# A graph layer on one core: the last but one node group's products behind the last pair's sum

## The chip, the cores and the metric

The kernel runs on one core of a Trainium2 chip. What counts is the time of one execution on the device, in microseconds (us), as the median of three runs. A separate execution was taken with the hardware profiler, and all readings of the trace come from it.

## The reference

One layer of graph attention (GATv2) with a feed-forward block, on 12,500 nodes of 128 features and 400,000 edges sorted by their destination. Every node has a self loop besides.

```python
h0 = relu(layernorm(x))
hn = LN(h0; ln1)
x_l, x_r, e = hn @ W_l, hn @ W_r, edge_attr @ W_e          # 8 heads of 16
m     = leaky_relu(x_l[src] + x_r[dst] + e, 0.2)           # a self loop's e is the mean over all edges
alpha = einsum(m, att)                                     # one score for each edge and head
a     = softmax of alpha over the edges of one destination
h     = h0 + segment_sum(x_l[src] * a, dst) + bias
out   = x + h + gelu(LN(h; ln2) @ W1 + b1) @ W2 + b2
```

All of it is in float32.

## The kernel before

A first stage computes the rows x_l for all nodes and puts them in DRAM. The main stage (window_edges) walks over the edges in 782 **pairs** of 512 edges (four tiles of 128; the last pair, 781, has one tile). Because the edges are sorted, a pair touches few nodes, and its result is a small record, rec, that is written with two DMAs into one of two state arrays in DRAM (L1073). Two writes into the same state array wait for each other.

The work of the main stage is written out by hand in **rounds**. Round r does one stage each of several pairs: GpSimd gathers the source rows xs of pair r + 4 (L926), one indirect DMA a tile; TensorE turns and sums pair r (combine, L980 and L984), starts the scores of pair r - 2 (apart, L991), turns the weights of pair r - 4 (L1033), sums pair r - 6 (collect, L1047) and ends the scores of pair r - 2 (score, L1008). VectorE takes the heads of pair r - 7 (own and rec, L1056 and L1062), the lowest score of pair r - 3 (L1014), the larger of z and its slope of pair r - 1 (m, L1003), and the places of pair r + 1 (ea and, every second round, ne, L967 and L973). ScalarE copies turned weights (L1038), slopes z (L998) and takes exponentials p (L1025). SP, which only issues DMAs, loads windows for pair r + 3 and writes the records of pair r - 7. Each engine works strictly in the order in which the code issues its instructions, and a waiting instruction holds all behind it on its engine. A few pairs are kept rows: their xs is loaded from late_dram by SP instead (pair 776 is the last of these).

PSUM has four rings of two banks each: z, ab, pt_ps and acc. An instruction that takes a new bank of a ring waits until the last use of the bank two before it is done. There are 12 buffers for xs.

Beside the pairs, the nodes are finished in **groups** of four tiles of 128 nodes (the first and the last have three), once the edges into them are done. A group's steps are: load its rows (f_load: three DMAs), self loop (f_order, f_z, f_bend, f_score, and f_kept, which copies the scores out of PSUM so that their bank comes free), read of both state arrays (f_state), weights (f_low, f_exp, f_den), weighted sum (f_out, which holds an ab bank until f_h is through), residual (f_h), statistics (f_stats, f_root, f_scale), turn (f_turn, f_turned), the two products and gelus (up0, up1, gelu0, gelu1), the product back (f_down), the result (f_store) and its DMA (f_put). A table for each kind of group says in which round, counted from the group's own, a step is issued: steps for all but the last two, which have one step a round; soon for the last but one, whose own round is 772; last_steps for the last, whose own round is 790, behind the last pair's sum in round 787 and its state writes in rounds 788 and 789.

f_biases adds the bias to h_sb and b2 to x ahead of time. In before only the last group has it; the others add them in f_h and in f_store. f_rest adds h_sb to x ahead of f_store, and f_ready is a Gelu of one column that makes ScalarE load the Gelu table early.

At the end of each round the tables are called in this order:

```python
in_round(r, steps, groups[:-2])
in_round(r, soon, groups[-2:-1])
in_round(r, last_steps, groups[-1:])
```

Of the kernel before, what the change touches and what calls it, by code (L numbers as in the profile page):

```python
# [851 lines left out]
def window_edges(  # L852
# [30 lines left out]
    with ExitStack() as es:  # L883
# [218 lines left out]
        groups = [{"t0": t, "n": n, "ts": slice(t, t + n)} for t, n in node_groups(NT)]  # L1102
        end = groups[-1]

        def own_tile(d, name, shape, dt, tag=None, bufs=1):

            if d is end and name in ("xo", "x", "sc"):
                return fin.tile(shape(d["n"]), dt, name=f"end_{name}")
            return fin.tile(shape(GN), dt, name=f"f_{name}", tag=tag or f"f_{name}", bufs=bufs)

        def tiles(name, d, tag=None):
            d[name] = own_tile(d, name, lambda n: [P, n, P], F32, tag)
            return d[name][:, 0 : d["n"]]

        def bank_of(d, name, ring="acc"):
            d[name] = ps2.tile([P, EPR], F32, name=ring)
            return d[name]
# [110 lines left out]
        def f_h(d):  # L1228
            hb = h_sb[:, d["ts"], :].rearrange("p t f -> p (t f)")
            nc.vector.tensor_add(d["sum"], d["sum"], d["o2"])  # L1230
            if d is not end:
                up = d["sum"].rearrange("p (t f) -> p t f", f=P)
                nc.vector.tensor_add(up, up, bias_r[:, None, :].to_broadcast([P, d["n"], P]))
            nc.vector.tensor_add(hb, hb, d["sum"])
# [31 lines left out]
                )  # L1266

        def f_turn(d):
            tp = bank_of(d, "tp")
            for i in range(d["n"]):  # L1270
                nc.tensor.transpose(tp[:, i * P : (i + 1) * P], d["hn"][:, i, :], ident)

# [20 lines left out]

        def f_up(k):
            def up(d):
                n, u = d["n"], bank_of(d, f"u{k}")
                nc.tensor.matmul(  # L1297
                    u[:, 0 : n * P],
                    w1_sb[:, k * P : (k + 1) * P],
                    d["hT"][:, 0:n].rearrange("p t f -> p (t f)"),  # L1300
                    start=True,
                    stop=True,
                )

            return up

        def f_gelu(k):
            def gelu(d):
                n = d["n"]
                if k == 0:  # L1310
                    d["gel"] = own_tile(d, "gel", lambda n: [P, 2, n * P], F32, "big", 3)
                nc.scalar.activation(
                    d["gel"][:, k, 0 : n * P], d[f"u{k}"][:, 0 : n * P], AF.Gelu, bias=cols[:, 5 + k : 6 + k]
                )

            return gelu

        def f_down(d):
            y = bank_of(d, "y")
            for i in range(d["n"]):  # L1320
                for k in range(2):
                    nc.tensor.matmul(  # L1322
                        y[:, i * P : (i + 1) * P],
                        d["gel"][:, k, i * P : (i + 1) * P],
                        w2_sb[:, k, :],
                        start=(k == 0),
                        stop=(k == 1),
                    )

        def f_store(d):  # L1330
            n = d["n"]
            up = d["y"][:, 0 : n * P].rearrange("p (t f) -> p t f", f=P)
            d["out"] = y = tiles("yo", d, "f_b")
            if d is end:
                nc.vector.tensor_add(y, up, d["x"][:, 0:n])
                return
            nc.vector.tensor_add(up, up, d["x"][:, 0:n])
            nc.vector.tensor_add(up, up, h_sb[:, d["ts"], :])
            nc.vector.tensor_add(y, up, b2_r[:, None, :].to_broadcast([P, n, P]))

        def f_put(d):
# [51 lines left out]
        )  # L1393
        up0, up1, gelu0, gelu1 = f_up(0), f_up(1), f_gelu(0), f_gelu(1)
        soon = (
            (-4, f_load),
            (-3, f_order),
            (-2, f_z),
            (-1, f_bend),
            (0, f_state),  # L1400
            (0, f_score),
            (1, f_low),
            (1, f_exp),
            (2, f_den),
            (2, f_out),
            (3, f_h),
            (3, f_stats),
            (4, f_root),
            (4, f_scale),
            (5, f_turn),  # L1410
            (5, f_turned),
            (6, up0),
            (6, gelu0),
            (7, up1),
            (7, gelu1),
            (8, f_down),
            (9, f_store),
            (9, f_put),
        )
        last_steps = (  # L1420
            (-18, f_load),
            (-17, f_order),
            (-16, f_z),
            (-15, f_bend),
            (-15, f_biases),
            (-14, f_score),
            (-13, f_kept),
            (0, f_state),
            (1, f_low),
            (1, f_exp),  # L1430
# [41 lines left out]
        with tc.manual_schedule():  # L1472
            for r in range(-AHEAD, max(last_round, groups[-1]["round"] + 18)):
                in_round(r, early, groups[:-2])
                for late, f in stages:
                    c = r - late
                    if 0 <= c < n_pr:
                        f(c)
                for late, f in sum_stages:
                    i, off = divmod(r - late, SUM_STEP)  # L1480
                    if off == 0 and 0 <= i < NL:
                        f(i)
                if r > 0 and r % CLEAR == 0 and r // CLEAR < NT // GT:
                    clear(r // CLEAR)
                in_round(r, steps, groups[:-2])
                in_round(r, soon, groups[-2:-1])
                in_round(r, last_steps, groups[-1:])
                in_round(r, enumerate(xr_steps), qs[1:])
                in_round(r, enumerate(raw_steps), raw)
                for late, f in late_stages:  # L1490
                    c = r - late
                    if 0 <= c < n_pr:
                        f(c)
# [354 lines left out]
```

## Time and profile before

| | us |
|---|---|
| median of 3 runs | 3979.37 (3976.93 to 3980.35) |
| profiled execution | 3979.82 |
| its span | 3978.0 |
| busy TensorE (matmul) | 3535.5 (89%) |
| busy VectorE | 2996.7 (75%) |
| busy GpSimd | 2961.1 (74%) |
| busy ScalarE | 2177.6 (55%) |
| mean granted clock of TensorE | 0.955 |

The 1.8 us between the profiled execution and its span lie outside what the profile shows. GpSimd's busy time leaves out the short pause before each gather. In the rows of a timeline the columns are start, duration, engine, line, operation, output and inputs, count, and in brackets the idle time before it and what ended it. In the rows of the chain that ended last they are start, duration and what the time went to. A stretch's row gives, for PE, PEld, DVE, ACT and POOL, the busy time and in brackets the instructions, then TensorE's granted clock, the DMA share and GB/s.

### The profile page before, as it was taken

What the parts mean: (1) busy time and instruction counts of PE and PEld (TensorE: products, weight loads), DVE (VectorE), ACT (ScalarE), POOL (GpSimd) and SP (SyncE); (2) the same over time, 40 slices, a digit from 0 to 9 for tenths busy, and PEclk for the clock granted to TensorE, in tenths of its full rate; (3) what the DMA queues carried; (4) which work ended last, traced back from release to release, by engine and by line L of the source; (5) the groups of instructions that cost most, each with busy time, mean ns of one, the idle gap of its engine ahead of it and who ended that gap; (6) DMA issues with size and microseconds to landing.
All of it is one profiled execution on the core that took longest, in us unless ns stands there. A gap on an engine that the chain in (4) does not pass through costs nothing.

```text
span 3978.0 us, 63158 instructions
## 1 busy us (share of the span) xinstructions
PE 3535.5 (89%) x18434; PEld 2235.4 (56%) x18435; DVE 2996.7 (75%) x6282; ACT 2177.6 (55%) x4746; POOL 2961.1 (74%) x3147
## 2 busy tenths in 40 slices
PE   2588899999999999999999999989999999999987
PEld 2355555555555556555665556656565655555554
DVE  6578888888878777777777777777777767767766
ACT  7445545555555545555555555556455555555554
POOL 7777777777777777777777777777777777777772
PEclk9799999999999999999999999999999999999998
DMA  7677777766655555555555555555555555555552
GB/s 207 210 176 175 182 190 179 165 161 154 151 103 114 109 112 112 109 110 108 104 110 115 109 110 111 113 109 108 112 104 107 110 115 97 110 110 100 107 104 63
DMA packets 625309, 502.69 MB, mean 126 GB/s; under 512 B 320174, under 2 KB 522013, under 8 KB 624717
## 3 DMA queue, kind: packets, MB, share of 16 engines
q1 hardware_dynamic: 524381, 281.11, 29.6%
q0 software_dynamic: 100000, 217.32, 27.7%
q8 instruction: 152, 2.49, 0.3%
q14 instruction: 200, 1.64, 0.1%
q10 hardware_dynamic: 576, 0.13, 0.0%
HBM read 432.27 MB, written 65.83 MB: 125 GB/s over the span
## 4 chain that ended last, share of the span: by engine, by line
PE 41%; POOL 20%; DMA 17%; issue 13%; DVE 7%; ACT 1%; SPq 1%; POOLq 0%; DVEq 0%; ACTq 0%
POOL xs L926 17%; DMA xs<-xl_dram,src_sb 14%; PE acc L1047 10%; PE z L984 10%; PE ab L1008 8%; PE pt_ps L1033 7%; PE z L980 4%; POOL raw L288 2%; DVE rec L1014 1%; DMA state<-rec 1%; DVE ea L967 1%; DVE m L1003 1%; PE acc L1322 1%; PE acc L1297 1%; DVE own L1056 1%
## 5 line engine op out<-in xcount | busy, mean ns | idle before, releaser
L926 POOL DMA_INDIRECT xs<-xl_dram,src_sb x3009 | 2842.4, 945 | 917.3 <-issue 790.1
L1025 ACT ACTIVATE p<-ab,rec 128x256 f32<-128x256 f32 x1563 | 654.8, 470 | 1026.9 <-DVE rec L1014 1011.6
L1047 PE MATMUL acc<-xs,pt 128*128 128x136 f32 x6250 | 904.6, 291 | 0.6 <-DVE f_m L1166 0.5
L984 PE MATMUL z<-ea,zw 64*128 64x512 f32 x1564 | 900.4, 656 | 3.8 <-DMA zw<-xr_dram 3.5
L980 PE MATMUL z<-ident,xs 128*128 128x128 f32 x3125 | 575.9, 285 | 291.0 <-DMA xs<-xl_dram,src_sb 260.3
L1056 DVE TENSOR_TENSOR own<-acc,diag 128x272 f32<-128x272 f32 x782 | 342.9, 438 | 652.5 <-PE acc L1047 646.5
L1008 PE MATMUL ab<-m,negrep 128*128 128x512 f32 x1564 | 833.5, 616 | 0.0
L1047 PEld LDWEIGHTS acc<-xs,pt 128*128 128x128 f32 x6250 | 828.8, 201 | 1.1 <-DVE f_m L1166 0.8
L980 PEld LDWEIGHTS z<-ident,xs 128*128 128x128 f32 x3125 | 406.9, 144 | 718.2 <-DMA xs<-xl_dram,src_sb 370.8
L1038 ACT COPY pt<-pt_ps 128x512 f32<-128x512 f32 x782 | 454.8, 582 | 573.1 <-PE pt_ps L1033 562.1
L1033 PEld LDWEIGHTS pt_ps<-ident,p 128*128 128x128 f32 x3125 | 340.5, 145 | 617.9 <-issue 510.1
L1003 DVE TENSOR_TENSOR m<-z,zs 128x512 f32<-128x512 f32 x782 | 532.8, 681 | 103.6 <-ACT zs L998 99.1
L967 DVE TENSOR_SCALAR ea<-dl,nid 32x516 f32<-32x516 bf16 x782 | 582.1, 744 | 29.0 <-DMA dl<-dc_dram 3.7
L1014 DVE TENSOR_REDUCE rec<-ab 128x2 f32<-128x512 f32 x781 | 538.8, 690 | 34.8 <-PE ab L1008 33.4
L1033 PE MATMUL pt_ps<-ident,p 128*128 128x128 f32 x3125 | 534.4, 296 | 2.6 <-ACT pt L1038 1.9
L998 ACT ACTIVATE zs<-z 128x512 f32<-128x512 f32 x782 | 472.0, 604 | 45.4 <-PE z L984 45.4
L1062 DVE TENSOR_REDUCE rec<-own 128x34 f32<-128x272 f32 x782 | 340.8, 436 | 26.7
L991 PE MATMUL ab<-ne,farw 64*128 64x512 bf16 x782 | 307.3, 393 | 31.2 <-ACT p L1025 27.4
L984 PEld LDWEIGHTS z<-ea,zw 64*128 64x128 f32 x1564 | 234.7, 188 | 122.3 <-issue 59.8
L1008 PEld LDWEIGHTS ab<-m,negrep 128*128 128x128 f32 x1564 | 252.8, 200 | 2.3 <-issue 2.3
L973 DVE TENSOR_SCALAR ne<-dl,nid 96x512 bf16<-96x512 bf16 x391 | 145.7, 373 | 12.7 <-DMA dl<-du_dram 0.3
L288 POOL DMA_INDIRECT raw<-in_x,src_raw x116 | 115.3, 994 | 38.8 <-issue 34.4
(206 smaller groups left out, 2163.2 us busy)
## 6 DMA issues: line engine op xcount, KB each, us to landing
ea<-in_ea_t SPq DMA_DIRECT2D x392, 128.0 KB
ea_s<-in_ea_t SPq DMA_DIRECT2D x98, 512.0 KB
xs<-xl_dram,src_sb POOLq DMA_INDIRECT x3009
dl<-dc_dram SPq DMA_DIRECT2D x392, 66.0 KB
state<-rec SPq DMA_DIRECT2D x1563, 9.0 KB
state<-empty SPq DMA_DIRECT2D x28, 504.0 KB
f_st<-state SPq DMA_DIRECT2D x46, 288.0 KB
dl<-du_dram SPq DMA_DIRECT2D x392, 32.0 KB
```

The source lines that it names most:

```text
L926: nc.gpsimd.indirect_dma_start(out=xs[:, j, :], out_offset=None, in_=xl_dram, in_offset=bass.IndirectOffsetOnAxis(ap=src_sb[:, c * KP + j ...
L967: nc.vector.tensor_scalar(d["ea"][rs].rearrange("p (a b) -> p a b", b=OW), d["dl"][rs].rearrange("p (a b) -> p a b", b=OS)[:, :, 0:OW], ni ...
L980: nc.tensor.matmul(z[:, j * P : (j + 1) * P], d["xs"][:, j, 0:P], ident, start=(j == 0), stop=False, is_transpose=True)
L984: nc.tensor.matmul(z[:, :e], d["zw"][rs], d["ea"][rs, :e], start=False, stop=True)
L998: nc.scalar.activation(d["zs"][:, :e], d["z"][:, :e], AF.Copy, scale=SLOPE)
L1003: nc.vector.tensor_tensor(d["m"][:, :e], d["z"][:, :e], d["zs"][:, :e], op=OP.max)
L1008: nc.tensor.matmul(d["ab"][:, :e], negrep.rearrange("p n h -> p (n h)"), d["m"][:, :e], start=False, stop=True)
L1014: nc.vector.tensor_reduce(d["rec"][:, :, CX], d["ab"].rearrange("p (u e) -> p u e", e=U), AX.X, OP.min)
L1025: nc.scalar.activation(d["p"][:, us], d["ab"][:, us], AF.Exp, bias=d["rec"][:, i, CX:SH], scale=-1.0)
L1033: nc.tensor.transpose(d["pt_ps"][:, js], d["p"][:, js], ident)
L1038: nc.scalar.copy(d["pt"][:, :e], d["pt_ps"][:, :e])
L1047: nc.tensor.matmul(d["acc"][:, i, :], d["pt"][:, j * P : (j + 1) * P], d["xs"][:, j, :], start=(j == js[0]), stop=(j == js[-1]),)
```

## The change

The last but one group (groups[-2]) changes its table. In soon, its loads and its self loop move from rounds 768 to 772 up to rounds 758 to 763, with f_biases and f_kept added; f_low stays in round 773; f_exp, f_den, f_out, f_h, f_stats, f_root and f_scale, which shared rounds 773 to 776 in twos and threes, get rounds 774 to 780, and f_rest is added in round 780. Its turn, products, gelus, product back, result and put leave rounds 777 to 781. They form a new table, after, and are counted from the last group's round 790: f_ready and the turn in round 788, the products and gelus in 789, f_down and f_store in 790, f_put in 791. Their PSUM banks come from the rings z and ab instead of acc. The last group's self loop moves from rounds 772 to 777 up to 764 to 769.

```diff
+        def near_end(d):
+            return any(d is g for g in groups[-2:])
+
...
-            if d is not end:
+            if not near_end(d):
                 up = d["sum"].rearrange("p (t f) -> p t f", f=P)
                 nc.vector.tensor_add(up, up, bias_r[:, None, :].to_broadcast([P, d["n"], P]))
...
-            tp = bank_of(d, "tp")
+            tp = bank_of(d, "tp", "z" if d is groups[-2] else "acc")
...
-                n, u = d["n"], bank_of(d, f"u{k}")
+                n, u = d["n"], bank_of(d, f"u{k}", "z" if d is groups[-2] else "acc")
...
-            y = bank_of(d, "y")
+            y = bank_of(d, "y", "ab" if d is groups[-2] else "acc")
...
-            if d is end:
+            if near_end(d):
                 nc.vector.tensor_add(y, up, d["x"][:, 0:n])
                 return
...
         soon = (
-            (-4, f_load),
+            (-14, f_load),
...
+        after = (
+            (-2, f_ready),
+            (-2, f_turn),
...
         last_steps = (
-            (-18, f_load),
+            (-26, f_load),
...
                 in_round(r, soon, groups[-2:-1])
+                for k, f in after:
+                    if end["round"] + k == r:
+                        f(groups[-2])
                 in_round(r, last_steps, groups[-1:])
```

In the changed kernel the lines below the new function are 3 higher, so that L1271, L1297, L1322 and L1342 are L1274, L1300, L1325 and L1345 there.

On TensorE, before, at the end of round 777 and over round 778, the turn (L1271) and the first product (L1297) stand between the pairs' instructions:

```order
5743 L1047 MATMUL acc<-xs,pt 128x136 x4
5744 L1008 MATMUL ab<-m,negrep 128x512
5745 L1271 MATMUL acc<-ident,f_hn 128x128 x4
5746 L980 MATMUL z<-ident,xs 128x128 x4
5747 L984 MATMUL z<-ea,zw_1772 128x512
5748 L991 LDWEIGHTS farw
5749 L991 MATMUL ab<-ne_1773,farw 128x512
5750 L1033 MATMUL pt_ps<-ident,p 128x128 x4
5751 L1047 MATMUL acc<-xs,pt 128x136 x4
5752 L1008 MATMUL ab<-m,negrep 128x512
5753 L1297 MATMUL acc<-f_hT,w_sb 128x512
```

On TensorE, after, at the end of the program:

```order
5783 L1033 MATMUL pt_ps<-ident,p 128x128 x4
5784 L1047 MATMUL acc<-xs,pt 128x136 x4
5785 L1033 MATMUL pt_ps<-ident,p 128x128
5786 L1047 MATMUL acc<-xs,pt 128x136 x9
5787 L1274 MATMUL z<-ident,f_hn 128x128 x4
5788 L1300 MATMUL z<-f_hT,w_sb 128x512 x2
5789 L1325 MATMUL ab<-w_sb,f_gel 128x128 x8
5790 L1274 MATMUL acc<-ident,f_hn 128x128 x3
5791 L1300 MATMUL acc<-f_hT,w_sb 128x384 x2
5792 L1325 MATMUL acc<-w_sb,f_gel 128x128 x6
```

The three rows of the four-tile group now stand between the last pairs' sums (L1047) and the last group's own three.

On SP, before, the put of the group (128x4x128) stands between the state writes, eight pairs from their end:

```order
4349 L1073 DMA state_69<-rec 128x72
4350 L1073 DMA state_70<-rec 128x72
4351 L1073 DMA state_69<-rec 128x72
4352 L1073 DMA state_70<-rec 128x72
4353 L1342 DMA out<-f_yo 128x4x128
4354 L1073 DMA state_69<-rec 128x72
4355 L1073 DMA state_70<-rec 128x72
```

On SP, after, at the end of the program:

```order
4367 L1073 DMA state_69<-rec 128x72
4368 L1073 DMA state_70<-rec 128x72
4369 L1073 DMA state_69<-rec 128x72
4370 L1126 DMA f_st<-state_69 128x3x144
4371 L1126 DMA f_st<-state_70 128x3x144
4372 L1345 DMA out<-f_yo 128x4x128
4373 L1345 DMA out<-f_yo 128x3x128
```

It has moved behind the last group's two state reads and stands right ahead of the last put.

On VectorE, after, at the end of the last pair's records, the group's result (L1338) now stands ahead of the last group's first step (L1190):

```order
6095 L1056 TENSOR_TENSOR own<-acc,diag 128x136
6096 L1062 TENSOR_REDUCE rec<-own 128x17
6097 L1338 TENSOR_TENSOR f_yo<-ab,f_x 128x512
6098 L1190 TENSOR_TENSOR f_mn<-f_st 128x24
6099 L1191 TENSOR_TENSOR f_mn<-f_mn,end_sc 128x24
```

In before it stood in three adds (L1337 to L1339) between the records of round 781.

More of the change, by code (lines that the diff above doesn't have):

```diff
@@ L1395, in window_edges @@
         soon = (
-            (-4, f_load),
-            (-3, f_order),
-            (-2, f_z),
-            (-1, f_bend),
+            (-14, f_load),
+            (-13, f_order),
+            (-12, f_z),
+            (-11, f_bend),
+            (-11, f_biases),
+            (-10, f_score),
+            (-9, f_kept),
             (0, f_state),
-            (0, f_score),
             (1, f_low),
[L1403 to L1418, printed above, removed]
+            (2, f_exp),
+            (3, f_den),
+            (4, f_out),
+            (5, f_h),
+            (6, f_stats),
+            (7, f_root),
+            (8, f_scale),
+            (8, f_rest),
+        )
+        after = (
+            (-2, f_ready),
+            (-2, f_turn),
+            (-2, f_turned),
+            (-1, up0),
+            (-1, up1),
+            (-1, gelu0),
+            (-1, gelu1),
+            (0, f_down),
+            (0, f_store),
+            (1, f_put),
         )
         last_steps = (
-            (-18, f_load),
[L1422 to L1427, printed above, removed]
+            (-26, f_load),
+            (-25, f_order),
+            (-24, f_z),
+            (-23, f_bend),
+            (-23, f_biases),
+            (-22, f_score),
+            (-21, f_kept),
             (0, f_state),
```

## Prediction

> **What bounds the kernel now.** The page first: GpSimd's gathers carry the loop.
>
> ```profile
> span 3978.0 us, 63158 instructions
> L926 POOL DMA_INDIRECT xs<-xl_dram,src_sb x3009 | 2842.4, 945 | 917.3 <-issue 790.1
> ```
>
> 945 ns busy and 917.3 / 3009 = 305 ns of idle before each make 1.25 us a gather, 5.0 us a pair of four. The timeline of GpSimd keeps that step to its end (columns: start, duration):
>
> ```profile
> 3895.36 0.94 POOL L926 DMA_INDIRECT xs<-xl_dram,src_sb  x1 [0.30 <-issue]
> ...
> 3915.62 0.94 POOL L926 DMA_INDIRECT xs<-xl_dram,src_sb  x1 [0.30 <-issue]
> 3916.87 0.94 POOL L926 DMA_INDIRECT xs<-xl_dram,src_sb  x1 [0.30 <-issue]
> ```
>
> These are the last gathers of pairs 775, 780 and 781 (pair 781 has one tile; pair 776 is a kept one that GpSimd doesn't gather). They never wait for a row tile. So nothing behind 3917.8 us can be won on GpSimd: 60.2 us of tail are left. How long a gather takes to land, from the chain that ended last:
>
> ```profile
> 3725.39 3.71 DMA xs<-xl_dram,src_sb
> ...
> 3885.37 5.41 DMA xs<-xl_dram,src_sb
> ```
>
> The second is pair 773: it lands at 3890.78, just as TensorE asks for it, so at round 773 TensorE has no arrears. Pair 781 lands at 3916.87 + 3.7 to 5.4 = 3920.6 to 3922.3. TensorE's timeline says when it is used:
>
> ```profile
> 3897.42 1.02 PE L1008 MATMUL ab<-m,negrep 128*128 128x512 f32 x2
> 3900.96 0.52 PE L1152 MATMUL acc<-ident,f_xl 128*128 128x128 f32 x3 [2.52 <-issue]
> ...
> 3918.52 0.63 PE L1271 MATMUL acc<-ident,f_hn 128*128 128x128 f32 x4 [2.33 <-DVE end_sc L1178]
> ...
> 3937.39 0.27 PE L980 MATMUL z<-ident,xs 128*128 128x128 f32 x1
> ...
> 3946.65 2.25 PE L1047 MATMUL acc<-xs,pt 128*128 128x136 f32 x18
> ```
>
> 3897.42 is the score that ends round 774; 3937.39 is pair 781's turn, 15 to 17 us behind its landing; the last sum ends at 3948.90 (call this moment S), 11.5 us later. So between 3890 and 3937 TensorE, not GpSimd, sets the end, and the arrears arise there: two stalls of 2.52 and 2.33 us while VectorE does the last but one group's steps, the group's own products, and a low clock, which the stretches show:
>
> ```profile
> 3920.00:3927.00 7.00, 7.00 (x18) 3.92 (x17) 3.01 (x5) 2.95 (x5) 0.00 (x0) 0.53 0.05 5
> ```
>
> TensorE is busy for all 7.00 us at a granted clock of 0.53: 7.0 x (1 - 0.53) = 3.3 us lost.
>
> **Part by part.** *Products moved behind the last sum.* Their steps in the chain that ended last:
>
> ```profile
> 3918.52 0.63 PE acc L1271 x4
> ...
> 3925.90 1.29 PE acc L1297 x2
> ...
> 3931.04 0.86 PE acc L1297 x2
> ...
> 3935.77 1.78 PE acc L1322 x16
> ```
>
> 0.63 + 0.86 + 0.86 + 1.78 = 4.13 us leave TensorE's path ahead of S (the 1.29 is the 0.86 at the low clock). With them two Gelu loads and the two Exp loads behind them leave ScalarE's rounds; ScalarE isn't what TensorE waits for there.
>
> *VectorE's steps, one a round instead of two or three.* These are VectorE's rows around the first stall (round 775 starts at 3900.78), and the last exponential of its round on ScalarE:
>
> ```profile
> 3893.76 0.44 DVE L1056 TENSOR_TENSOR own<-acc,diag 128x272 f32<-128x272 f32 x1 [0.88 <-PE acc L1047]
> 3896.72 0.28 DVE L1201 TENSOR_TENSOR f_ws<-f_wt,f_st 128x64 f32<-128x64 f32 x1
> 3898.25 0.70 DVE L1214 TENSOR_TENSOR ab<-f_st,acc 128x512 f32<-128x512 f32 x1
> 3900.78 0.43 DVE L1056 TENSOR_TENSOR own<-acc,diag 128x272 f32<-128x272 f32 x1
> 3902.31 0.84 ACT L1025 ACTIVATE p<-ab,rec 128x256 f32<-128x256 f32 x2 [4.54 <-DVE rec L1014]
> 3903.95 0.69 DVE L1230 TENSOR_TENSOR ab<-ab,f_o 128x512 f32<-128x512 f32 x1
> ```
>
> A round's own work takes 2.96 us (3893.76 to 3896.72), or 3.17 in the rounds that also place ne (3900.78 to 3903.95); f_den 1.53; f_out 2.53; from a round's start to its last p it is 3903.15 - 3900.78 = 2.37. In before, f_den and f_out together stand between two rounds (4.06 us). Apart they fit better, but f_out still puts 2.53 us into round 776. It also takes an ab bank, so that apart of round 777 must wait for p of round 777. An earlier group, whose steps already come one a round, shows this very wait, and what followed:
>
> ```profile
> 3754.31 0.60 PE L980 MATMUL z<-ident,xs 128*128 128x128 f32 x4
> 3758.32 0.37 PE L991 MATMUL ab<-ne,farw 64*128 64x512 bf16 x1 [2.36 <-ACT p L1025]
> 3760.67 1.91 PE L1008 MATMUL ab<-m,negrep 128*128 128x512 f32 x2
> 3762.38 0.81 PE L980 MATMUL z<-ident,xs 128*128 128x128 f32 x4
> 3765.59 1.02 PE L1008 MATMUL ab<-m,negrep 128*128 128x512 f32 x2
> 3769.45 1.02 PE L1008 MATMUL ab<-m,negrep 128*128 128x512 f32 x2
> ```
>
> A free round takes 3769.45 - 3765.59 = 3.86 us. That one took 3762.38 - 3754.31 = 8.07: 3.86 + 2.36 of waiting + 1.85 at a low clock (the score took 1.91 instead of 1.02).
>
> Now the rounds of after. Round 774 as before, its score done at 3898.3. Round 775 waits for its pair, 3895.36 + 3.7 to 5.4 = 3899.1 to 3900.8; from a landing to the end of a round it is a free round, so it ends at 3903.0 to 3904.7. Round 776 has its pair: 3906.9 to 3908.5. VectorE enters round 776 with the sum of 775, 0.86 before that round's end, at 3902.1 to 3903.8; + 3.17 + 2.53 it enters 777 at 3907.8 to 3909.5, and p is there at + 2.37: 3910.2 to 3911.9. TensorE reaches apart some 0.9 us into its round 777, at 3907.8 to 3909.4, and waits 2.4 to 2.5 us, as the earlier group did. The round then needs another 2.97 (3.86 - 0.9): 3913.2 to 3914.9. Three rounds of 3.86 bring pair 781's turn to 3924.8 to 3926.4; its landing by 3922.3 doesn't hold it. Against 3937.39 that is 11.0 to 12.6 us earlier, and 9.1 to 10.7 if the low clock takes 1.85 again. From there to S the same pairs have the same 11.5 us of TensorE.
>
> [...]
>
> *Self loops of both groups earlier* (rounds 758 to 769): six loads past state writes and window loads on SP, two copies, two ScalarE slopes, two f_m, four bias adds on VectorE, two f_z and f_score on TensorE, and one f_kept more. I cost them at nothing: there TensorE waits for gathers, at most this long:
>
> ```profile
> 3863.54 0.33 PE L980 MATMUL z<-ident,xs 128*128 128x128 f32 x1 [1.90 <-DMA xs<-xl_dram,src_sb]
> ...
> 3880.80 1.06 PE L1156 MATMUL acc<-ident,f_xr 128*128 128x128 f32 x8
> ```
>
> and it gets back rounds 770 to 776, which lose their f_z (about 1.5 us for four tiles) and f_score. If that cover is gone, arrears of some us come into round 774; a free round gains 5.0 - 3.86 = 1.1 us on the gathers.
>
> *Behind S.* What the moved group must not delay:
>
> ```profile
> 3948.25 0.43 DVE rec L1062
> ...
> 3948.94 1.43 DMA state<-rec
> ```
>
> ```profile
> 3953.52 0.93 SPq L1123 DMA_DIRECT2D f_st<-state  x2
> ...
> 3956.88 0.20 DVE L1187 TENSOR_TENSOR f_mn<-f_st 128x24 f32<-128x24 f32 x1 [6.72 <-DMA f_st<-state]
> ```
>
> f_mn starts 8.0 us after S, after three state writes one behind the other, the first 0.26 us behind its rec: SP has caught up with what its wait on f_put had held, so taking that wait away gives nothing. The moved chain, from S: turn 0.63, f_hT, two products of 0.86, the second gelu, the second half of L1322 at most 1.78, one add:
>
> ```profile
> 3919.18 0.78 ACT L1286 ACTIVATE f_hT<-acc,cols 128x512 f32<-128x512 f32 x1 [0.61 <-PE acc L1271]
> ...
> 3932.35 0.69 ACT L1312 ACTIVATE f_gel<-acc,cols 128x512 f32<-128x512 f32 x1
> ...
> 3937.77 0.69 DVE L1337 TENSOR_TENSOR acc<-acc,f_x 128x512 f32<-128x512 f32 x1
> ```
>
> 0.63 + 0.78 + 1.72 + 0.69 + 1.78 + 0.69 = 6.3, with some 0.04 at each handing on 6.6. f_mn, queued behind that add on VectorE, has 1.4 us to spare; at half the clock TensorE's 4.13 us more would take 2.7 of it too much. The clock is still full there:
>
> ```profile
> 3953.00:3954.00 1.00, 0.00 (x0) 0.00 (x0) 0.00 (x0) 0.00 (x0) 0.00 (x0) 0.97 0.03 2
> ```
>
> it falls only 5 us after S. The Exp load lies in the same gap on ScalarE. f_put stands behind the state loads on SP and holds only the last put. The rest of the tail, 21.1 us from f_mn, keeps its order. Two adds of f_store and one of f_h are gone from VectorE (0.69 each); no wait of TensorE hangs on them.
>
> Sum: 11.8 us (middle of 11.0 to 12.6), less 1.85 for the low clock = 9.95. The profiled run takes 3979.82 (span and 1.8 around it), 0.45 over the median of 3979.37: 3979.82 - 9.95 - 0.45 gives a median of 3969.4.
>
> **The rivals.**
>
> - *No low clock.* The 2.4 us wait passes as the 2.52 us one did: 3979.4 - 11.8 = 3967.6. For it one idle in three; against it the closest twin.
> - *A longer loss.* The low clock lasts as in 3920 to 3927 (3.3 us), or pair 780 lands late, or VectorE stays behind: gain 7 to 8.5, time 3971 to 3972.5.
> - *Only the products are won.* The stalls come back at other rounds, as arrears from rounds 758 to 772: gain 4.13, time 3975.2. For it: VectorE works 9.59 of the 10 us at 3900, in this row, and its sum of work hardly falls:
>
> ```profile
> 3900.00:3910.00 10.00, 8.50 (x50) 5.76 (x51) 9.59 (x25) 2.39 (x5) 7.55 (x9) 1.00 0.29 62
> ```
>
> - *Slower.* The loads and VectorE steps at rounds 758 to 769 hold TensorE so long that GpSimd finds no free row tile (12 of them, filled 4 rounds ahead, emptied 6 rounds behind), and its last gather slips. Each us it stands costs one us of the end; it decides only once it passes the 10 us won, and slower by 8 us needs 18, some 3.6 pairs. Against it: GpSimd's idle stays at 0.30 even beside the low clock near 3866. Time 3987 and up.
> - *No change:* the moved chain holds f_mn at half the clock (2.7 us) and rival three holds too: 3978.
>
> **How the numbers follow.** Three runs differ by 3.4 us, and 0.2% is 8.0 us, about what a measurement can tell. Forecast 0.42, no low clock 0.26, longer loss 0.13 (half of it over 8.0), only products 0.11, slower 0.05, no change 0.03. Faster: 0.42 + 0.26 + 0.06 = 0.74; same: 0.07 + 0.11 + 0.03 = 0.21; slower 0.05. The range runs from 3966.0, where apart of round 777 would wait for nothing (11.0 + 2.4 = 13.4 us), to 3975.5, which takes in the third rival.
>
> **What would show it.** GpSimd's last gather still at 3916.9; pair 781's L980 at 3925 to 3928; one wait of L991 on p near 3908; the low clock, if any, right behind it and none at 3920; S at 3936 to 3939; f_yo's add done before f_st lands, f_mn 8 us after S. I am wrong if GpSimd's end moves, if f_mn comes later than 8.3 us after S, or if TensorE waits for VectorE in rounds 778 to 781.

## The result and the profile after

The changed kernel takes 3971.46 us (median; 3967.20 to 3974.63), the kernel before 3978.16 us beside it on the same chip (3975.27 to 3981.08), 21 times each. The medians are 6.7 us apart (0.17 %); the ratio of the runs is 0.9981 with an interval of 0.9975 to 0.9987. The profiled execution took 3973.0 us, its span is 3971.2 us.

On the page GpSimd's gathers are what they were:

```profile
span 3971.2 us, 63157 instructions
...
L926 POOL DMA_INDIRECT xs<-xl_dram,src_sb x3009 | 2843.4, 945 | 917.4 <-issue 772.6
```

TensorE's timeline of the changed kernel from round 777 on (start, duration, and in brackets the idle time before):

```profile
3908.80 0.60 PE L980 MATMUL z<-ident,xs 128*128 128x128 f32 x4
...
3912.99 0.37 PE L991 MATMUL ab<-ne,farw 64*128 64x512 bf16 x1 [2.54 <-ACT p L1025]
...
3915.45 1.91 PE L1008 MATMUL ab<-m,negrep 128*128 128x512 f32 x2
3917.16 0.70 PE L980 MATMUL z<-ident,xs 128*128 128x128 f32 x4
...
3928.85 0.27 PE L980 MATMUL z<-ident,xs 128*128 128x128 f32 x1
...
3938.11 2.25 PE L1047 MATMUL acc<-xs,pt 128*128 128x136 f32 x18
```

Neither stall of before is left. One wait stands in their place, that of apart in round 777 on p, and the score behind it takes 1.91 us as in the earlier group that served as the model. That round lasts 3917.16 - 3908.80 = 8.36 us. Pair 781's turn comes 8.54 us earlier than before, and S (the end of the last pair's sum) is at 3940.36 instead of 3948.90. Where the stretch from 3920 to 3927 had a granted clock of 0.53, it is now full (the clock is the number behind the five engines):

```profile
3920.00:3927.00 7.00, 7.00 (x38) 4.10 (x37) 6.47 (x19) 4.73 (x9) 0.00 (x0) 1.00 0.10 15
```

GpSimd's last gather, which the prediction held fixed at 3916.87, starts here:

```profile
3918.70 0.94 POOL L926 DMA_INDIRECT xs<-xl_dram,src_sb  x1 [0.30 <-issue]
```

Behind S, VectorE's timeline shows the moved group's add and the last group's first step:

```profile
3946.29 0.69 DVE L1338 TENSOR_TENSOR f_yo<-ab,f_x 128x512 f32<-128x512 f32 x1 [4.68 <-PE ab L1325]
3948.28 0.20 DVE L1190 TENSOR_TENSOR f_mn<-f_st 128x24 f32<-128x24 f32 x1 [1.30 <-DMA f_st<-state]
```

The add is done 6.62 us after S and f_mn starts 7.92 after S, still released by the state reads. Up to here the tail is as forecast. From f_mn to the end it isn't: it takes 3971.2 - 3948.28 = 22.92 us instead of 21.12. ScalarE's timeline, first before, then after:

```profile
3958.13 1.28 ACT L1251 ACT_TABLE_LOAD   x1
...
3964.29 0.20 ACT L1251 ACTIVATE f_rstd<-f_rstd 128x3 f32<-128x3 f32 x1 [4.88 <-DVE f_rstd L1248]
```

```profile
3955.58 1.28 ACT L1254 ACT_TABLE_LOAD   x1 [6.22 <-DVE f_rstd L1251]
3956.88 0.20 ACT L1254 ACTIVATE f_rstd<-f_rstd 128x3 f32<-128x3 f32 x1
```

Before, the load of the Sqrt table ran 6 us ahead of its root and was hidden. After, the load itself waits for VectorE's f_rstd, and its 1.28 us lie on the path. From VectorE's f_rstd to the root it is 1.54 us instead of 0.20, so 1.34 of the 1.8 us. The last products take 0.69 us more (the first row is of before, the second of after), and 0.23 us are saved at other steps of the tail:

```profile
3971.10 1.38 PE L1322 MATMUL acc<-w_sb,f_gel 128*128 128x128 f32 x10 [0.24 <-ACT f_gel L1312]
```

```profile
3963.68 2.07 PE L1325 MATMUL acc<-w_sb,f_gel 128*128 128x128 f32 x10 [0.24 <-ACT f_gel L1315]
```

The sum between the two profiled spans: pair 781's turn moves from 20.52 us behind the last gather to 10.15 (-10.37), the last gather is 1.83 later, and S to the end takes 30.84 instead of 29.10 us (+1.74): -6.80.

### The profile page after: what moved, and what is told of

It reads as the page before. It is cut to its first block, busy times and chain, and to the rows that moved or that the text cites. A ratio compares the mean times of both kernels' runs of the same rounds, so it can differ in the third digit from the quotient of the medians.

```text
span 3971.2 us, 63157 instructions
## 1 busy us (share of the span) xinstructions
PE 3530.8 (89%) x18434; PEld 2230.9 (56%) x18435; DVE 2996.5 (75%) x6283; ACT 2174.7 (55%) x4745; POOL 2961.7 (75%) x3147
## 4 chain that ended last, share of the span: by engine, by line
PE 41%; POOL 20%; DMA 16%; issue 13%; DVE 7%; SPq 1%; ACT 1%; POOLq 0%; DVEq 0%; ACTq 0%
POOL xs L926 18%; DMA xs<-xl_dram,src_sb 14%; PE acc L1047 10%; PE z L984 10%; PE ab L1008 8%; PE pt_ps L1033 7%; PE z L980 4%; POOL raw L288 2%; DVE rec L1014 1%; DVE ea L967 1%; DVE m L1003 1%; PE acc L1325 1%; DMA state<-rec 1%; PE acc L1300 1%; DVE own L1056 1%
## 5 line engine op out<-in xcount | busy, mean ns | idle before, releaser
L1047 PE MATMUL acc<-xs,pt 128*128 128x136 f32 x6250 | 904.4, 290 | 0.0
L1056 DVE TENSOR_TENSOR own<-acc,diag 128x272 f32<-128x272 f32 x782 | 342.6, 438 | 654.7 <-PE acc L1047 647.4
L1047 PEld LDWEIGHTS acc<-xs,pt 128*128 128x128 f32 x6250 | 828.9, 201 | 0.0
```

The lines of the kernel that those rows point to most:

```text
L1047: nc.tensor.matmul(d["acc"][:, i, :], d["pt"][:, j * P : (j + 1) * P], d["xs"][:, j, :], start=(j == js[0]), stop=(j == js[-1]),)
```

## The experiments

The kernels ran in three groups, each on one chip beside the kernel before. In the first group before takes 3978.98 us, in the third 3980.40. The second group's chip is slower altogether (before 4772.64 us), so only its ratios are used.

### First group: the wait on p, the table load, the products alone

**f_ready reads a constant.** In the changed kernel f_ready of the moved group reads f_rstd on ScalarE. The theory was that this read makes the next root's table load wait for f_rstd.

```diff
         def f_ready(d):
-            nc.scalar.activation(own_tile(d, "mn", ...)[:, 0:1], d["rstd"][:, 0:1], AF.Gelu)
+            src = cols[:, 2:3] if d is groups[-2] else d["rstd"][:, 0:1]
+            nc.scalar.activation(own_tile(d, "mn", ...)[:, 0:1], src, AF.Gelu)
```

> The changed kernel, but the one-column Gelu that loads the table for the moved group (f_ready) reads a column of constants instead of f_rstd. Theory (the last group's Sqrt table load has taken over a wait, since f_rstd has a second reader on ScalarE): the load stands right behind f_exp again, f_rstd comes 0.2 us behind its VectorE step and not 1.54 us, and the run is 1.3 us shorter than the changed kernel, 8.0 us under before. Rival (the load was late for another reason, such as the order of the tables): the load still ends 1.5 us behind f_rstd's VectorE step, and the time is the changed kernel's, 6.7 us under before.

Median 3971.19 us (3967.27 to 3974.41), ratio 0.998 (0.9971 to 0.9989). ScalarE's timeline of this kernel:

```profile
3948.53 1.28 ACT L1254 ACT_TABLE_LOAD   x1
3954.70 0.20 ACT L1254 ACTIVATE f_rstd<-f_rstd 128x3 f32<-128x3 f32 x1 [4.88 <-DVE f_rstd L1251]
```

The load is off the path again, and the root starts 0.2 us after VectorE's f_rstd (3954.50) instead of 1.54. So it is f_ready's read of f_rstd that makes the load late; by what means, no row shows. 1.3 us are too few to be seen in medians of runs that differ by 7 us. The table of tails below sees them.

**f_out's sum in SBUF.**

```diff
         def f_out(d):
-            d["sum"] = bank_of(d, "sum", "ab")[:, 0 : n * P]
+            if d is groups[-2]:
+                d["sum"] = fin.tile([P, EPR], F32, name="f_sum")[:, 0 : n * P]
+            else:
+                d["sum"] = bank_of(d, "sum", "ab")[:, 0 : n * P]
```

> The changed kernel, but the weighted sum of the last but one group lies in SBUF instead of a bank of the ring ab. Theory (f_out's step costs TensorE the 2.54 us wait for p in round 777 through that bank, and the low clock of 1.96 us follows from the wait): both go, pair 781's turn comes 3.5 to 4.5 us earlier against the last gather, limited by the landing of pairs 780 and 781, and the run is 10 to 11 us under before. Rival (VectorE's 2.5 us in that round are what holds TensorE, whichever memory the sum lies in): the wait moves to the next apart, score or collect and the time stays 6.7 us under before.

Median 3970.19 us (3967.92 to 3972.83), ratio 0.9978 (0.9969 to 0.9987): 8.8 us under before, less than expected. TensorE's timeline:

```profile
3915.50 0.33 PE L980 MATMUL z<-ident,xs 128*128 128x128 f32 x1 [1.04 <-DMA xs<-xl_dram,src_sb]
...
3919.10 0.49 PE L980 MATMUL z<-ident,xs 128*128 128x128 f32 x3
3920.60 0.33 PE L980 MATMUL z<-ident,xs 128*128 128x128 f32 x1 [1.01 <-DMA xs<-xl_dram,src_sb]
...
3924.19 0.27 PE L980 MATMUL z<-ident,xs 128*128 128x128 f32 x1
```

The wait on p and the low clock are gone (the granted clock is 1.00 in each of the stretches from 3900 to 3927). TensorE now waits for the gathers of pairs 779 and 780, and pair 781's turn comes 5.73 us behind the last gather: the arrears are gone altogether. So the wait in round 777 was the ab bank's, as predicted.

**The products alone.** Self loops and VectorE's steps go back to before's rounds; turn, products and gelus stay behind the last sum.

```diff
         soon = (
-            (-14, f_load),
...
-            (8, f_scale),
+            (-4, f_load),
+            (-3, f_order),
+            (-2, f_z),
+            (-1, f_bend),
+            (-1, f_biases),
             (0, f_state),
+            (0, f_score),
...
+            (2, f_den),
+            (2, f_out),
...
         last_steps = (
-            (-26, f_load),
+            (-18, f_load),
...
```

> One part alone: the turn, products, gelus, result and put of the last but one group stand behind the last pair's sum, but the self loops of both groups and VectorE's steps of rounds 773 to 776 stay in the rounds of before (with f_biases and f_rest for the group). Theory: 4.1 us of products leave the path, the stalls of about 2.5 and 2.3 us and the low clock behind them stay, and the tail gives back 1.3 us (late Sqrt load): 2 to 4 us under before. Rival (the products are the whole gain): 6.7 us under before.

Median 3973.39 us (3971.94 to 3979.08), ratio 0.9986 (0.9976 to 0.9995): 5.6 us won, more than the 2 to 4 expected, where TensorE's work that moved is 4.13 us (the interval takes in both). The profiled execution is the slowest of the eleven, 3979.08 us, so its profile is not that of a typical execution. Rows of TensorE's timeline and a stretch:

```profile
3905.97 0.52 PE L1155 MATMUL acc<-ident,f_xl 128*128 128x128 f32 x3 [2.50 <-issue]
...
3934.05 0.27 PE L980 MATMUL z<-ident,xs 128*128 128x128 f32 x1
```

```profile
3907.00:3914.00 7.00, 7.00 (x23) 4.41 (x22) 6.69 (x19) 2.40 (x5) 5.47 (x6) 0.51 0.39 66
```

The first stall is there, with a low clock behind it; the second, 2.33 us at f_turn, went with the turn, which had not been expected.

**Before again, one execution.**

> The kernel before once more, for a second profile of it. Theory (the last gather's issue differs between executions of the same program): the last gather starts within 2 us of 3916.87, not at the same time, the two stalls of rounds 774 and 777 come again at 2.3 to 2.6 us, and the low clock may come at other places. Rival (the gathers' end is fixed by the program): the last gather starts at 3916.9 within 0.2 us.

3979.77 us, span 3978.0. Both stalls stand again (2.16 us at 3901.71, 2.34 at 3919.40), the last gather starts at 3917.75, and the last products take 2.30 us instead of 1.38. So 0.9 us of the last gather and 0.9 us of the last products differ between two executions of one kernel.

### Second group, on the slower chip

The first kernel joins the first two edits above. The second is before's kernel with only the last group's self loop moved (its steps from -18 to -13 go to -26 to -21). The third is the first edit with the group's turn, products, result and put left out of the table after, so that 512 rows of the output are not written. The fourth is the changed kernel, one execution.

> Both repairs together: f_ready reads a constant, and the sum of the last but one group lies in SBUF. From the last gather's issue to the end of the span it was 60.2 and 59.3 us in the two profiles of before, 51.6 in the changed kernel, 49.6 with the constant alone, 46.8 with the sum in SBUF alone. Theory (two separate terms that add up): 1.3 us less than with SBUF alone, 45.0 to 46.5 us, and a median 9 to 12 us under before. Rival (the gain of the one is taken up by the other, since the Sqrt load then waits for VectorE anyway): 46.8 us again.

> One part alone, on the kernel before: only the last group's self loop moves up by 8 rounds (764 to 769). Theory: its f_z, f_m, two bias adds and f_score (1.2, 1.5 and 0.7 us) leave rounds 774 to 776, but f_den and f_out still stand together in round 774 and the products stay: from the last gather to the end 56.5 to 59 us against 60.2 and 59.3, time 1 to 3 us under before. Rival (this part holds most of the 2 us by which the changed kernel beats the products-only kernel): no more than 2 us, with the 2.5 us wait of round 774 gone. Rival (no gain): 59.3 to 60.2 us.

> The kernel with the constant for f_ready, and the last but one group's turn, products, gelus, result and put left out altogether: its 512 rows of the output stay unwritten. Theory (behind the last sum they are wholly hidden by the state round trip): from the last sum's end to f_mn 7.9 to 8.0 us as with them, from the last gather to the end 49 to 50 us, the same as with them (49.6). Rival (they still hold the end by something that the chain doesn't show, such as their 256 KB put beside the last group's loads or TensorE's clock): 1 us or more shorter than 49.6.

> The changed kernel once more, for a second profile. Theory: from the last gather to the end 50 to 52.5 us again, with one wait of 2.3 to 2.6 us on p and the Sqrt load on the path; the last gather itself anywhere from 3916 to 3922. Rival (the changed rounds 758 to 769 slow the gathers): the last gather again 1.5 us or more behind 3916.9 and 3917.8, and the last 124 gathers, from about round 750 on, take longer than in before by as much.

| kernel | us | ratio to before |
|---|---|---|
| constant and SBUF sum | 4764.82 | 0.9982 (0.9973 to 0.9991) |
| last group's loop early | 4767.14 | 0.9990 (0.9981 to 1.0000) |
| without the products | 4763.91 | 0.9983 (0.9974 to 0.9992) |
| changed kernel, one execution | 4765.44 | - |

These can't be told apart by time. The chip has waits of its own inside rounds, which the trace puts to nothing; this is a row of the changed kernel there:

```profile
4696.18 1.97 PE L1047 MATMUL acc<-xs,pt 128*128 128x136 f32 x8 [3.68 <-issue]
```

Its last 60 gathers took 91.5 us instead of 75.7. Two readings can be taken all the same. Without the moved products it takes 29.94 us from S to the end, of which the last ten products take 2.41; with them, in the kernel of both edits, 29.45 and 1.90. That leaves 27.53 and 27.55: the moved work costs the tail nothing. And with the last group's loop early, the second stall is gone though the turn stands where it stood:

```profile
4699.85 1.02 PE L1008 MATMUL ab<-m,negrep 128*128 128x512 f32 x2
4700.70 0.60 PE L1271 MATMUL acc<-ident,f_hn 128*128 128x128 f32 x4
```

So the turn alone does not make the second stall, as the run with the products alone had suggested. That led to the third group.

### Third group: the self loops alone, the change without the spread

**The self loops alone.** Before's kernel, with the loops of both groups in the changed kernel's rounds.

```diff
         soon = (
-            (-4, f_load),
-            (-3, f_order),
-            (-2, f_z),
-            (-1, f_bend),
+            (-14, f_load),
+            (-13, f_order),
+            (-12, f_z),
+            (-11, f_bend),
+            (-10, f_score),
+            (-9, f_kept),
             (0, f_state),
-            (0, f_score),
...
         last_steps = (
-            (-18, f_load),
+            (-26, f_load),
...
```

> Before's kernel with one part of the change alone: the self loops of the last two groups (loads, z, bend, score, the score's copy to SBUF) in the changed kernel's rounds 758 to 769; the products and VectorE's later steps stay where they were. The prediction cost this move at nothing: then the median lies within 1.5 us of before, GpSimd's last gather starts at 3916.9 to 3917.8 as in the two profiles of before, and the waits of 2.2 to 2.5 us near 3901 and 3919 remain. First rival: the move slows the gathers, which the profiles of the changed kernel end 0.9 to 1.8 us later: 1 to 2 us slower than before, last gather at 3918.5 or later. Second rival: taking f_z and f_score out of rounds 770 to 777 frees TensorE there: 3 to 5 us under before, as the one run with the last group's loop alone suggested (0.1 % under before, not settled).

Median 3976.44 us (3974.25 to 3979.28) against 3980.40: 4.0 us won by the medians, as the second rival had it, ratio 0.9993 (0.9984 to 1.0002). The interval of the ratio doesn't rule out that nothing is won; the trace is clearer, with pair 781's turn 14.60 us behind the last gather instead of 20.52 and 18.83 in the two profiles of before. TensorE's timeline:

```profile
3904.53 0.37 PE L991 MATMUL ab<-ne,farw 64*128 64x512 bf16 x1 [2.88 <-ACT p L1025]
...
3916.52 0.60 PE L1271 MATMUL acc<-ident,f_hn 128*128 128x128 f32 x4
...
3932.32 0.27 PE L980 MATMUL z<-ident,xs 128*128 128x128 f32 x1
```

Both stalls are gone with the loops alone. In before, the rows on VectorE that ended just ahead of the two starts are these:

```profile
3900.18 0.68 DVE L1214 TENSOR_TENSOR f_o<-f_xo,acc 128x512 f32<-128x512 f32 x1
...
3918.20 0.17 DVE L1178 COPY end_sc<-acc 128x24 f32<-128x24 f32 x1
```

The first stall (L1152, at 3900.96) is the last group's own f_z, which asks for an acc bank right after f_den has taken one, and gets it only when VectorE is through f_out. The profile names no releaser for it, but L1152 starts 0.10, 0.09 and 0.10 us behind the end of f_out's last step in the three profiles that have the stall (before, before again, the products alone). It can't have waited for the bank two before, with pair 768's sum: VectorE still reads that one (L1056, 3900.78 to 3901.21) when L1152 starts. The second is the turn waiting for the acc bank of the last group's f_score, which VectorE empties late (f_kept). Without the loops there, neither is asked for. What is left of the first is the ab bank: VectorE is as late as before, now apart waits 2.88 us for it in round 775, with a low clock behind it (L1047 takes 2.02 us instead of 1.09). Nothing else slipped: the last gather starts at 3917.72.

**The change without the spread.** The changed kernel with f_den and f_out in one round, 774, and so on, as before (the expectation counts these rounds one too high).

```diff
-            (2, f_exp),
-            (3, f_den),
-            (4, f_out),
-            (5, f_h),
-            (6, f_stats),
-            (7, f_root),
-            (8, f_scale),
+            (1, f_exp),
+            (2, f_den),
+            (2, f_out),
+            (3, f_h),
+            (3, f_stats),
+            (4, f_root),
+            (4, f_scale),
```

> The changed kernel without the spreading of VectorE's steps: f_exp in round 774, f_den and f_out together in 775, f_h and f_stats in 776, f_root and f_scale in 777, as before; self loops early and products behind the last sum as in the changed kernel. If the spread matters, TensorE waits some 2.5 us near 3901 to 3906 and again at the bank, and the median is 1 to 2.5 us over the changed kernel's of this call. If the gain is the products' and the second wait's alone (the theory after the run with the products alone, which was 5.6 us under before against 6.7 for the whole change), it is the changed kernel's within 1 us.

Median 3974.64 us (3972.58 to 3976.01), ratio 0.9985 (0.9976 to 0.9994). TensorE's timeline:

```profile
3906.23 0.37 PE L991 MATMUL ab<-ne,farw 64*128 64x512 bf16 x1 [3.26 <-ACT p L1025]
...
3929.82 0.27 PE L980 MATMUL z<-ident,xs 128*128 128x128 f32 x1
```

Round 775 lasts 9.30 us (3901.20 to 3910.50): a free round's 3.86, the wait of 3.26, and 2.18 more, by estimate the low clock behind it.

**Constant and SBUF sum, and the changed kernel,** beside before on the same chip.

> The changed kernel with f_ready reading a constant and with f_out's sum in an SBUF tile, on another chip than before if the queue gives one. Theory: no wait on p, no low clock, TensorE waits for the last gathers alone; S about 5 us sooner after the last gather than in the changed kernel, and the Sqrt's table load is off the path (1.3 us): tail from the last gather to the end 45 to 46 us instead of 51.6, so 4 to 6 us under the changed kernel's median and 10 to 13 under before. Rival: the gathers end later by what TensorE gives them to fight for (the last 60 took 76.6 us in the run with the SBUF sum against 75.2 to 75.7 elsewhere), which takes 1 to 2 us of it: 2 to 4 under the changed kernel. Third: no difference, within 1.5 us of the changed kernel.

> The changed kernel itself, as the yardstick for the three others of this call: 6.7 us (0.17 %) under before, ratio 0.9975 to 0.9987 as measured. Its profile should show the wait of apart on p near 2.5 us, the low clock behind it, the table load behind f_rstd, and GpSimd's last gather at 3917 to 3919 if its later end is chance, at 3918.4 to 3919 again if the change makes it.

The changed kernel: 3972.51 us (3970.91 to 3976.87), ratio 0.9984 (0.9975 to 0.9993). With the two edits: 3970.25 us (3968.39 to 3971.77), ratio 0.9976 (0.9967 to 0.9985). It beats before by 10.2 us and the changed kernel by 2.3 (drawing anew from the 11 times of each, 1.2 to 4.1). The changed kernel without the spread is 2.1 us slower than with it, by the same drawing 0.1 to 2.6.

TensorE's and GpSimd's timelines of the kernel with both edits:

```profile
3922.77 0.63 PE L980 MATMUL z<-ident,xs 128*128 128x128 f32 x4 [0.49 <-PE ab L1008]
...
3926.83 0.27 PE L980 MATMUL z<-ident,xs 128*128 128x128 f32 x1
```

```profile
3921.33 0.94 POOL L926 DMA_INDIRECT xs<-xl_dram,src_sb  x1 [0.30 <-issue]
```

Pair 781's turn follows the last gather by 5.50 us, near the floor (the prediction's landing takes 3.7 to 5.4), but that gather itself is 4.46 us later than in before's profile. So the gain over the changed kernel is the rival's (2 to 4), not the 4 to 6 of the theory.

### All profiles of the first and third group side by side

From each trace: the start of GpSimd's last gather; pair 781's turn behind it; S to the end of the span; of that, the last ten products; and what is left.

| kernel | last gather | turn behind it | S to end | last products | rest |
|---|---|---|---|---|---|
| before | 3916.87 | 20.52 | 29.10 | 1.38 | 27.72 |
| before again | 3917.75 | 18.83 | 29.92 | 2.30 | 27.62 |
| loops alone | 3917.72 | 14.60 | 29.07 | 1.59 | 27.48 |
| products alone | 3921.90 | 12.15 | 31.74 | 2.50 | 29.24 |
| without the spread | 3919.77 | 10.05 | 30.38 | 1.51 | 28.87 |
| changed | 3918.70 | 10.15 | 30.84 | 2.07 | 28.77 |
| changed again | 3919.02 | 9.25 | 30.63 | 1.77 | 28.86 |
| constant | 3918.78 | 9.09 | 29.92 | 2.23 | 27.69 |
| SBUF sum | 3918.46 | 5.73 | 30.50 | 1.49 | 29.01 |
| constant and SBUF sum | 3921.33 | 5.50 | 29.53 | 1.84 | 27.69 |

The last column falls into two classes: 27.5 to 27.7 where the table load is hidden, 28.8 to 29.2 where f_ready of the moved group reads f_rstd. Their means are 27.64 and 28.95, 1.31 us apart, for 1.34 us of load and root in ScalarE's rows; with the constant the moved products stand behind S and the tail is before's. The last products vary from 1.38 to 2.50 us without order among the kernels (1.38 and 2.30 in before's own two profiles), with the clock: it is at 0.50 for a stretch behind S (from 3953.94 in before, from 3951.49 in the changed kernel) and is full again at 3971.01 in before, just ahead of their start at 3971.10, but only at 3965.15 in the changed kernel, 1.47 us behind their start at 3963.68. The 0.69 us by which the changed kernel lost there is chance.

Of the last gather's 1.83 us, 1.27 are there at gather 2900, far ahead of the first moved row (round 758 is some 75 gathers from the end), and the second profile of before is 1.04 later there too. From that gather to the last, the changed kernel's two profiles lose 0.56 and 0.44 us on before, the constant 0.25, without the spread 0.29; before again and the loops alone gain 0.16 and 0.36; the products alone and both kernels with the SBUF sum lose 1.24 to 1.62. So some half a microsecond seems to come with the change and a microsecond more with the SBUF sum, from one or two profiles of each kernel. In GpSimd's rows the pauses are the same, at most 0.31 us; the loss is in one to six single gathers of these 110 that take longer than 0.96 us. Over the usual 0.94 they add up to 0.5 us in before, 1.1 and 0.9 in the changed kernel, and 1.9 and 2.1 with the SBUF sum. What makes them long stays open.

## Why the prediction was right or wrong

The forecast was 3969.4 us and 0.74 for a gain over 0.2 %; measured are 3971.46 us and a gain of 0.13 to 0.25 %, around 0.19 by the ratio and 0.17 by the medians, so the likelier side is just under that bound. The range (3966.0 to 3975.5) holds it and the direction is right. The time is 2.1 us above the forecast, but the gain falls 3.3 us short of it (6.7 instead of 10.0): before's median over 21 runs is 1.2 us under the one over three that the forecast started from.

- **The stalls and the clock, as one sum: right.** Forecast were one wait of apart in round 777 of 2.4 to 2.5 us and 1.85 us of low clock; the trace has 2.54 and 8.36 - 3.86 - 2.54 = 1.96. Against the last gather the turn was to stand 3937.39 - 9.95 - 3916.87 = 10.57 us later; it stands at 10.15 and 9.25. In the time of the span it stands at 3928.85 and S at 3940.36, outside the 3925 to 3928 and 3936 to 3939 that were to show it, because the last gather is 1.83 us later.
- **The low clock behind the wait: right.** The clock fell after waits of 2.54, 2.50 and 2.33 us, and after one of 1.86 (the rows of the changed kernel's second profile stand in the last section). That it cost 1.96 us here and not the 3.3 of before was taken over from the earlier group, not derived, and is partly luck.
- **"Self loops of both groups earlier ... I cost them at nothing": wrong.** They give 4.0 us by themselves by the medians, 4.2 to 5.9 by the turn against the last gather. The step that failed is the one ahead of it: the two stalls were put to VectorE's packed steps, which ran beside the first and ended the second. What was waited for were two acc banks that the last group's self loop itself asked for or held.
- **"VectorE's steps, one a round": oversized.** Both stalls and the low clock were charged to it, some 5.8 us of the 9.95. With the loops moved its own worth is 2.1 us by the medians (0.1 to 2.6). The traces show part of it: the round with the wait on p takes 8.36 and 7.77 us instead of 9.30, but against the last gather the turn stands at 10.15 and 9.25 for 10.05 without the spread. What the spread would do with the loops in their old rounds, no run shows.
- **The products: right in kind, not additive.** Against the last gather, the turn gains 14.60 - 10.05 = 4.55 us from the kernel with the loops alone to the one without the spread, for 4.13 forecast. By the clock the products alone win 5.6, the loops alone 4.0 and both 5.8: each of the two takes the second stall away, and it can be taken away once.
- **"The rest of the tail, 21.1 us from f_mn, keeps its order": wrong by 1.34 us.** The order of the instructions is kept, the waits aren't: with f_ready, added for this group with the table after, the table load of the Sqrt's root takes over the root's wait on VectorE, and with a constant in f_ready it doesn't. Of the loads the working looked at the Exp's alone there and did not go through f_ready. The load takes 1.28 us in the trace and the root starts 0.02 us behind it, so the switch cost 1.3 us here.
- **"GpSimd's last gather still at 3916.9": wrong, mostly by chance.** It starts 1.83 us later, of which 1.27 were there ahead of the first moved row. Two executions of before differ by 0.9 us in it; some 0.5 us may be the change's.
- **SP: right.** Behind f_put's removal nothing was won, f_mn is 7.92 us after S for 8.0 forecast. The moved chain took 6.62 us for 6.6 forecast, at a granted clock of 1.00.

The rival of a longer loss names the time that was measured (3971 to 3972.5), but not its cause: the low clock lasted as in the forecast, and pair 780 did not land late. Between the two profiled spans the gain is 6.80 us for 9.95 forecast: the last gather is 1.83 us later and the tail 1.74 longer (1.34 of it the table load), while the stretch between them wins 10.37, 0.42 more than forecast. The late gather and the slower last products differ from one execution to the next; the table load doesn't.

## What to carry to other kernels

A profile names at best the instruction that ended a wait, not what was asked for: before costing a move, find which buffer the waiting instruction wanted and who had taken it, because a step that is itself cheap and early may hold the ring. When one part of a change removes a stall that another part also removes, the parts don't add up, so each wants a run alone. And a small early activation can put a later table load on the path: f_ready, which read an old tile, cost 1.3 us of load in the tail, and reading a constant instead took it off again.

## What the runs showed of the hardware that was not expected

The low clock does not follow from the length of the wait alone. It came after 1.86 us in the changed kernel's second profile, where weights, sums and score take 1.08, 2.02 and 1.42 us instead of 0.66, 1.09 and 1.02:

```profile
3912.43 0.37 PE L991 MATMUL ab<-ne,farw 64*128 64x512 bf16 x1 [1.86 <-ACT p L1025]
3912.73 1.08 PE L1033 MATMUL pt_ps<-ident,p 128*128 128x128 f32 x4
3913.61 2.02 PE L1047 MATMUL acc<-xs,pt 128*128 128x136 f32 x8
3915.42 1.42 PE L1008 MATMUL ab<-m,negrep 128*128 128x512 f32 x2
```

It came after 2.50 us with the products alone and stayed for 7 us at 0.51, and it did not come after 2.52 us at the same instruction in before, nor after 2.16 in before again (the sum behind it, L1047, takes 1.09 us). What goes with the difference in the traces is where the wait lies. In the profiles of before and of the changed kernel the recorded low spells start whole multiples of 3.41 us apart, to within 0.01 us, and last one or more steps of that length at a clock of 0.50 (the last one is cut off by the end). At 3.41 x (1 - 0.50) a step, a spell of one step costs about 1.7 us and one of two steps 3.4, an estimate that is near the 1.96 of the changed kernel and the 3.3 of before. These are such steps in before, around its two stalls:

```profile
3895.92:3899.31 3.39, 2.52 (x15) 1.62 (x14) 3.10 (x8) 1.34 (x3) 2.48 (x4) 1.00 0.50 70
3899.33:3902.72 3.39, 1.76 (x14) 1.62 (x16) 3.32 (x7) 0.41 (x2) 2.60 (x3) 1.00 0.28 67
3902.74:3906.14 3.40, 3.40 (x20) 2.11 (x19) 3.23 (x7) 1.97 (x5) 2.68 (x3) 1.00 0.42 74
...
3916.40:3919.79 3.39, 1.27 (x10) 1.14 (x11) 3.25 (x7) 2.75 (x5) 1.11 (x2) 1.00 0.35 54
3919.81:3923.20 3.39, 3.39 (x12) 1.94 (x10) 1.44 (x2) 3.14 (x6) 0.00 (x0) 0.50 0.05 5
```

The wait of 2.52 us is cut in two by the end of a step, with TensorE idle for 0.87 and 1.63 us, and the clock stays at 1.00. Of the 2.33 us of the second stall 2.12 lie in one step, and the next step runs at 0.50. In the changed kernel TensorE idles for 2.46 us in the step of its wait, and the next runs at 0.50 too:

```profile
3910.54:3913.95 3.41, 0.95 (x7) 0.75 (x8) 3.31 (x8) 0.84 (x2) 2.50 (x4) 1.00 0.58 114
3913.96:3917.36 3.40, 3.40 (x11) 2.26 (x11) 2.03 (x4) 1.08 (x2) 2.57 (x3) 0.50 0.34 68
```

Between 100 and 3948 us of these two profiles, a full-clock step in which TensorE idled for 2.0 us or more was followed by a low one in all 46 cases, and one with less than 0.75 us in none of 1730; of the 290 between the two, 77 were. Why some spells last two steps although TensorE is busy stays open, and no row shows what sets the clock.

The moment at which GpSimd issues its last gather differs by 5 us between profiles (3916.87 to 3921.90), though the pauses between its gathers are 0.3 us throughout; 3.8 of the 5 us are there at gather 2900, before the changed rounds begin.
